# A four-layer graph network in fp32: order of messages and their sums in layers one, three and four

## The chip, the cores and the metric

The kernel runs on one core of one Trainium2 chip. The metric is device time in microseconds (us); the time before is the median of three runs. Inputs and outputs lie in the chip's memory (HBM), and everything is computed in fp32. Engines are named as the profile names them: PE (TensorE), with PEld for its weight loads, DVE (VectorE), ACT (ScalarE), POOL (GpSimd) and SP (SyncE, which issues most DMAs).

## The reference

Sixteen graphs of 1024 nodes with 128 features each go through a graph convolution, a residual and a layer norm, then through a network of four layers, a residual and a layer norm. The four-layer part is what the change is about:

```python
def _layer(nodes, adj, ws, bs, wd, bd, wn, bn, wu, bu):
    src = nodes @ ws + bs
    src_agg = jnp.einsum('bjv,bij->biv', src, _l2norm(adj, 2))
    dst = nodes @ wd + bd
    dst_agg = jnp.einsum('bjv,bji->biv', dst, _l2norm(adj, 1))
    self_rep = nodes @ wn + bn
    upd = jnp.concatenate([src_agg, self_rep, dst_agg], axis=2)
    return jnp.tanh(upd @ wu + bu)
...
for i in range(NUM_LAYERS):
    if i < half:
        stashed.append(fpass)
    elif i == half:
        fpass = jnp.concatenate([fpass, stashed[NUM_LAYERS - i - 1]], axis=2)
    else:
        fpass = jnp.concatenate([fpass, stashed[NUM_LAYERS - i], stashed[NUM_LAYERS - i - 1]], axis=2)
    fpass = _layer(fpass, adj, *params[i])
```

Each node sends a source and a destination message, which are summed over the neighbours with the adjacency matrix (once as it is and once transposed, each normed by rows or columns). The input of layers three and four is two and three blocks of 128 features.

## The kernel before

**Work and order.** The graphs are worked through one after the other, and each engine's order is the order in which the code issues (the scheduling is by hand). While layers one to four of graph b run on TensorE, the other engines prepare graph b+1: they load its adjacency, form its sums of squares, scale and transpose it, and run its first convolution (`first_gnn`) between layers three and four. These pieces hang in `hooks` (issued before a given matmul of `aggregate`) and `between` (issued at numbered places of the messages). The layers are numbered `l` = 0 to 3 in the code, so "layer one" is `l == 0`, "layer three" `l == 2`, "layer four" `l == 3`.

**Messages.** A layer first makes its messages: for each of the eight blocks of 128 nodes the features are the stationary operand and the folded weights stream. They are kept in two SBUF tiles, `t0` (nodes' blocks 0 to 3) and `t1` (blocks 4 to 7). Layers one and two do it in `messages` (L684): a group `g` is two blocks, its product fills one PSUM bank, and DVE evicts it with the bias at L696. The groups come in the order 2, 3, 0, 1, so `t1` is filled first. Layers three and four do it in `paired_messages` (L722), with seven products in place of eight (a Winograd scheme): M4, M1, M2, M3, Z11, Z12 and Z21, where T2, T3 and T4 are differences of halves of the features (L719, L761, L764), and DVE combines the banks at L752, L755 and L758.

**Sums.** The aggregation uses the same seven-product scheme, and for it needs sums of the messages, made by `message_sums` (L702): with X[v, j] the half v of the features in tile `t`j, S3 = X[0,0] - X[1,0], then S1 = X[1,0] + X[1,1], which is written over X[1,0], then S2 = S1 - X[0,0] and S4 = X[0,1] - S2. Every one has a destination part (DST) and a source part (SRC), 256 elements a partition each. S3 is made as two instructions, one for each part (L708), the others as one (L709, L710, L711).

**Aggregation.** `aggregate` (L852) writes its matmuls (L1003) as two lists, `upper` and `lower`, for the upper and the lower 64 columns of the array, and issues them in turn. Each list runs through accumulators in PSUM: in layer one, after products of the node's own features, `upper` begins with M1 (accumulator A, operands X[0,0]) and `lower` with M3 (accumulator Dk, operand S3), then M4 (Ck, S1). In layer four, after the own products, `upper` takes two blocks of M1 and then M2 (Bk, S2), and `lower` two blocks of M4 (S1) and then M3 (S3). In layer three M3 and M4 come after two blocks of Z11. The own products of layers three and four use T2, T3 and T4 once more.

**Buffers.** Four PSUM banks (tag `pt`) serve the messages' products and the accumulators Ck, Dk, A and Bk in rotation. In `messages` all four are filled and evicted in order, and in layer one `aggregate` then takes them in the order Ck, Dk, A, Bk; an accumulator's first matmul waits until the eviction that last read its bank is done. In SBUF, layers three and four keep two scratch tiles, `e0` and `e12` (two halves, `e12[:, 0]` and `e12[:, 1]`). There is one buffer of `e0` for all layers, and the one before layer three is still read by the last tanh of layer two (L1021). T2 lies in `e12[:, 1]`, T4 in `e12[:, 0]`, T3 in `e0`; after the messages and own products, the aggregation uses the tiles for its own results.

**Order of layer three's messages before.** Place 0 (for all graphs but the first and last the three small operations of `inverse_rows`, L395 to L398), M4 and its copy on ACT (L773), M1 and its eviction with bias (L758), then T3 (L761), T4 (L764), then Z12, M2, M3 and the rest.

**Things behind the sums of layer four.** On DVE: `ve` (L452) of the next graph's first norm, which POOL's power (L454) waits for, L459 after that, the next graph's T operations (L680, L676, L678), and the transposes of its rows (L653), the last of which stand right before the evictions of the next graph's layer one.

Of the kernel before, what the change touches and what calls it, by code (L numbers as in the profile page):

```python
# [8 lines left out]
F32 = mybir.dt.float32  # L9
# [5 lines left out]
P = 128  # L15
# [8 lines left out]
def adj_resnorm_kernel(ctx: ExitStack, tc: tile.TileContext, x, adj, w0, b0, layers, out):  # L24
# [33 lines left out]
    nc = tc.nc  # L58
    B, N, D = x.shape
    NB = N // P  # L60
    HW = 512
# [4 lines left out]
    NQ = 4  # L66
# [37 lines left out]
    one = ctx.enter_context(tc.tile_pool(name="one", bufs=1))  # L104
# [38 lines left out]
    def message_seven(wm):  # L143
        return seven(wm, (wm, MSUMS), 2 * P, P)
# [165 lines left out]
    def degree_of(a, state, i, engine=nc.scalar):  # L310
        degree = state["cols"][:, 2 * NB + i:2 * NB + i + 1]
        if engine is nc.vector:
            nc.vector.reduce_sum(degree, a[:, i, :], axis=AX.X)
        else:
# [25 lines left out]
    def column_reduce(b, state, tr):  # L340
        part = two.tile([P, K], F32, tag="part", name=f"part{b}")
        nc.vector.reduce_sum(part, tr.rearrange("p (k r) -> p k r", r=C), axis=AX.X)
        state["part"] = part
# [178 lines left out]
    def first_quarter_3(b, y, T2):  # L522
        T3 = []
        for j in range(2):
# [157 lines left out]
    SRC, DST = 0, 1  # L682

    def messages(b, l, feats, wm, between={}, with_sums=True):  # L684


        nch = CHUNKS[l]
        t = [one.tile([P, NJ, 2, 2, V], F32, tag=f"t{j}", name=f"t{l + 1}_{b}_{j}") for j in range(2)]
        for n, g in enumerate((2, 3, 0, 1)):
            pt = ps_t.tile([P, 2, 2 * P], F32, tag="pt", name=f"pt{l + 1}_{b}_{g}")  # L690
            for q in range(2):
                i = 2 * g + q
                for k, (f, c) in enumerate(feats):
                    by_halves(pt[:, q], f[:, i * P:(i + 1) * P], wm[:, 1 + c], k == 0, k == nch - 1)
            j, o = divmod(2 * g, NJ)
            nc.vector.tensor_add(t[j][:, o:o + 2].rearrange("p k a v c -> p k (a v c)"), pt,  # L696
                                 wm[:, 0][:, None, :].to_broadcast([P, 2, 2 * P]))
            if n in between:
                between[n]()
        return message_sums(b, l, t) if with_sums else t  # L700

    def message_sums(b, l, t):  # L702

        S = {i: one.tile([P, NJ, 2, V], F32, tag=f"S{i}", name=f"S{i}_{l + 1}_{b}") for i in (2, 3, 4)}
        X = {(v, j): t[j][:, :, :, v] for v in range(2) for j in range(2)}
        S[1] = X[1, 0]
        for part in (DST, SRC):
            nc.vector.tensor_sub(S[3][:, :, part], X[0, 0][:, :, part], X[1, 0][:, :, part])  # L708
        nc.vector.tensor_add(S[1], X[1, 0], X[1, 1])  # L709
        nc.vector.tensor_sub(S[2], S[1], X[0, 0])  # L710
        nc.vector.tensor_sub(S[4], X[0, 1], S[2])  # L711
        return X, S

    def begin_paired(b, l, first, second, etag):

        e12 = one.tile([P, 2, HW], F32, tag=etag, name=f"e12_{l}_{b}")
        y = {(j, h): f[:, half(h)] for j, f in enumerate((first, second)) for h in range(NH)}
        w = {"e12": e12, "y": y, "T2": e12[:, 1], "T4": e12[:, 0]}
        nc.vector.tensor_sub(w["T2"], y[1, 1], y[0, 1])  # L719
        return w  # L720

    def paired_messages(b, l, w, wm, rest=None, between={}):  # L722

        t = [one.tile([P, NJ, 2, 2, V], F32, tag=f"t{j}", name=f"t{l + 1}_{b}_{j}") for j in range(2)]
        X = {(v, j): t[j][:, :, :, v] for v in range(2) for j in range(2)}
        y, s, T2, T4 = w["y"], message_seven(wm), w["T2"], w["T4"]
        T3 = w["e0"] = one.tile([P, HW], F32, tag="e0", name=f"e0_{l}_{b}")
        o = own_seven(l, wm)
        w["own"] = {"M1": (o["w00"], y[0, 0]), "M2": (o["S2"], T2), "M3": (o["S3"], T3), "M4": (o["S1"], y[0, 1]),
                    "Z11": (o["w01"], y[1, 0]), "Z12": (o["S4"], y[1, 1]), "Z21": (o["w11"], T4)}  # L730

        def bank(i):
            return product(f"pt{l + 1}_{b}_{i}")

        def parts(pt):
            return pt.rearrange("p (k a c) -> p k a c", k=NJ, a=2)

        def into(pt, *terms):
            for i, (f, x) in enumerate(terms):
                for k in range(NJ):  # L740
                    by_halves(pt[:, k * P:(k + 1) * P], f[:, k * P:(k + 1) * P], x, i == k == 0,
                              i == len(terms) - 1 and k == NJ - 1)
            return pt

        def plain(v, h):
            return [(rest[:, half(h)], wm[:, MREST + v * P:MREST + (v + 1) * P])] if rest is not None else []

        def bias(v):
            return wm[:, v * P:(v + 1) * P].rearrange("p (a c) -> p a c", a=2)[:, None].to_broadcast([P, NJ, 2, V])

        def add(to, x, pt):
            nc.vector.tensor_add(X[to], X[x], parts(pt))  # L752

        def add_sbuf(to, x):
            nc.vector.tensor_add(X[to], X[to], X[x])  # L755

        def add_bias(to, x, v):
            nc.vector.tensor_add(X[to], x, bias(v))  # L758

        def t3():  # L760
            nc.vector.tensor_sub(T3, T2, y[0, 0])  # L761

        def t4():
            nc.vector.tensor_sub(T4, y[1, 0], T2)  # L764

        def at(i):
            if i in between:
                between[i]()

        if l == 2:  # L770
            at(0)
            m4 = into(bank(4), (y[0, 1], s["S1"]))
            nc.scalar.copy(X[1, 1], parts(m4))  # L773
            m1 = into(bank(1), (y[0, 0], s["w00"]))
            add_bias((0, 0), parts(m1), 0)
            t3()
            t4()
            z12 = into(bank("z12"), (y[1, 1], s["S4"]))
            m2 = into(bank(2), (T2, s["S2"]))
            at(1)  # L780
            add((0, 1), (0, 0), m2)
            m3 = into(bank(3), (T3, s["S3"]))
            add((1, 0), (0, 1), m3)
            add_sbuf((0, 1), (1, 1))
            at(2)
            add((0, 1), (0, 1), z12)
            z11 = into(bank("z11"), (y[1, 0], s["w01"]))
            add((0, 0), (0, 0), z11)
            z21 = into(small(f"pt{l + 1}_{b}_z21", [HW]), (T4, s["w11"]))
            add_bias((1, 0), X[1, 0], 1)  # L790
            add_sbuf((1, 1), (1, 0))
            add((1, 0), (1, 0), z21)
        else:
            t4()
            t3()
            m4 = into(bank(4), (y[0, 1], s["S1"]))
            nc.scalar.copy(X[1, 1], parts(m4))
            at(0)
            m1 = into(bank(1), (y[0, 0], s["w00"]))
            add_bias((0, 0), parts(m1), 0)  # L800
            at(1)
            m2 = into(bank(2), (T2, s["S2"]))
            add((0, 1), (0, 0), m2)
            at(2)
            z11 = into(bank("z11"), (y[1, 0], s["w01"]), *plain(0, 0))
            m3 = into(bank(3), (T3, s["S3"]))
            add((1, 0), (0, 1), m3)
            add_bias((1, 0), X[1, 0], 1)
            z12 = into(bank("z12"), (y[1, 1], s["S4"]), *plain(0, 1))
            add_sbuf((0, 1), (1, 1))  # L810
            at(3)
            add((0, 0), (0, 0), z11)
            add_sbuf((1, 1), (1, 0))
            add((0, 1), (0, 1), z12)
            z21 = into(small(f"pt{l + 1}_{b}_z21", [HW]), (T4, s["w11"]), *plain(1, 0))
            add((1, 0), (1, 0), z21)
            p11 = into(bank("p11"), *plain(1, 1))
            add((1, 1), (1, 1), p11)
            at(4)
        XS = message_sums(b, l, t)  # L820
        if l == 2:
            at(3)
        return XS

    def plain_layer(b, l, feats, t, wm, a, at, fT, etag, hooks):
# [279 lines left out]
    wm = message_tile("wm1_0")  # L1105
# [10 lines left out]
    wm = as_chunks(wm, 0)  # L1116
# [11 lines left out]
    for p in (3, 4):  # L1128
        v = one.tile([P, NJ, HW], F32, tag=f"T{p}", name=f"sq0_{p}").rearrange("p k i -> p (k i)")
# [131 lines left out]
    for b in range(B):  # L1261
        nxt = b + 1 < B
        n = b + 1
        y, yt = quarters(a), quarters_t(at)
# [5 lines left out]
        if b == 0:  # L1270
# [17 lines left out]
            t = messages(b, 0, feats, wm, {0: second_x1, 1: factors_and_fold, 2: row_factors0}, with_sums=False)  # L1288
# [47 lines left out]
            wm = message_weights(b, 1)  # L1336
            a2 = load(n)
            xs2 = load_spread(n)
        else:
            w = {}  # L1340
            if nxt:
                st = begin_sums(n)
            t = messages(b, 0, feats, wm)
# [30 lines left out]
            wm = ahead["wm"]  # L1374
# [5 lines left out]
        t = messages(b, 1, feats, wm)  # L1380
# [23 lines left out]
        else:  # L1404
            nm = f"1_{b - 1}"
            w = {"ys": summed(f"y{nm}", "xa")}
# [34 lines left out]
        wm = ahead["wm"]  # L1441
# [5 lines left out]
        w = {}  # L1447
# [54 lines left out]
        t = paired_messages(b, 2, p, wm, None, between)  # L1502
# [9 lines left out]
        wm = ahead["wm"]  # L1512
# [8 lines left out]
        if nxt:  # L1521
            nm = f"0_{n}"
            xT2 = w["xT"]
            w = {}
# [102 lines left out]
        t = paired_messages(b, 3, p, wm, f23, between)  # L1627
        if nxt:
            wm = message_weights(n, 0)
# [10 lines left out]
    b = B - 1  # L1640
# [48 lines left out]
```

## Time and profile before

| what | value |
|---|---|
| median of three runs | 2396.12 us (2395.91 to 2396.41) |
| the profiled execution's own time | 2395.86 us |
| its span, first to last instruction | 2394.1 us |
| granted TensorE clock | 0.999 |
| matmuls of the aggregation, L1003, in the chain that ended last | m 40%, z 28%, m3s 1% of the span |
| matmuls of the messages, L245, in that chain | pt 9%, pt_z 5%, pt_p 1% |
| DVE in that chain | 1% |
| mean of one L709, L710 or L711 (128x512) | 692 ns |
| mean of one L708 (128x256) | 420 ns |
| mean of one L696 eviction (128x512 out of PSUM) | 684 ns |
| mean of one power on POOL, L454 | 6396 ns |

The span is the profiler's; the time is the run's own, 1.8 us longer. Busy time of PE is a union of matmuls whose ends are modelled, so it is read together with the start times. In the timeline a line merges consecutive instructions of one kind: start of the first, time to the end of the last, their number, and in brackets the engine's idle time before it with what ended it. A line of the stretches gives the length, then for each engine its busy time and number of instructions.

### The profile page before, as it was taken

How to read it: one execution, taken by the hardware profiler on the slowest of the kernel's cores; microseconds unless marked ns; L12 is line 12 of the kernel's file. 1: busy time of each engine (PE TensorE's matmuls, PEld its weight loads, DVE VectorE, ACT ScalarE, POOL GpSimd, SP SyncE). 2: the span in 40 equal slices, each digit the busy share in tenths (PEclk: the TensorE clock that was granted, in tenths of full speed). 3: DMA queues.
4: the chain of work that ended last, by engine and by line, in shares of the span. 5: the costliest groups of instructions: out<-in, count | busy, mean ns of one | idle time of the engine just before them, and what ended most of it. 6: DMA issues, size and time to landing. Idle time of an engine off the chain costs nothing.

```text
span 2394.1 us, 39329 instructions
## 1 busy us (share of the span) xinstructions
PE 2377.4 (99%) x15289; PEld 1279.6 (53%) x15289; DVE 2092.6 (87%) x2817; ACT 980.8 (41%) x1845; POOL 275.8 (12%) x103
## 2 busy tenths in 40 slices
PE   8999999999999999999999999999999999999998
PEld 4444564645556455554655546456464554645555
DVE  6998888999889989889988889888898988998954
ACT  5425345253343524435244452434525344352322
POOL 4101111001111011110111110111100111101110
PEclk9999999999999999999999999999999999999999
DMA  9527244262533627335272442634427253362400
GB/s 205 124 75 147 69 115 90 70 148 57 135 78 81 138 48 157 61 97 115 55 163 55 108 97 71 147 69 110 91 70 151 57 133 76 80 141 48 100 22 22
DMA packets 363387, 232.03 MB, mean 97 GB/s; under 512 B 150353, under 2 KB 334306, under 8 KB 363202
## 3 DMA queue, kind: packets, MB, share of 16 engines
q1 hardware_dynamic: 362386, 227.03, 42.5%
q0 software_dynamic: 816, 2.49, 0.4%
q8 instruction: 121, 1.98, 0.4%
q14 instruction: 64, 0.52, 0.1%
HBM read 209.59 MB, written 19.84 MB: 96 GB/s over the span
## 4 chain that ended last, share of the span: by engine, by line
PE 92%; DVE 1%; issue 0%; POOLq 0%; ACT 0%; DVEq 0%
PE m L1003 40%; PE z L1003 28%; PE pt L245 9%; PE pt_z L245 5%; PE m_f L581 5%; PE z_f L581 2%; PE pw L245 2%; PE m3s L1003 1%; PE pt_p L245 1%; DVE t L752 0%; PE pv L250 0%; PE pm L250 0%; DVE f L534 0%; PE rp L250 0%; DVE t L758 0%
## 5 line engine op out<-in xcount | busy, mean ns | idle before, releaser
L1003 PE MATMUL m<-a,t 128*64 128x512 f32 x1008 | 434.7, 593 | 0.2 <-DVE t L709 0.2
L1003 PE MATMUL m<-at,t 128*64 128x512 f32 x1008 | 418.6, 592 | 0.0
L1003 PE MATMUL m<-Q,S 128*64 128x512 f32 x880 | 394.0, 593 | 0.0
L1003 PE MATMUL m<-T,S 128*64 128x512 f32 (+1 forms) x1040 | 393.6, 573 | 0.0
L454 POOL TENSOR_TENSOR rs<-ve,mhalf 128x32 f32<-128x32 f32 x30 | 191.9, 6396 | 988.4 <-DVE ve L452 988.4
L1003 PE MATMUL z<-at,t 128*64 128x512 f32 x504 | 229.2, 592 | 0.0
L1003 PE MATMUL z<-at,S 128*64 128x512 f32 x504 | 228.3, 593 | 0.0
L1003 PE MATMUL z<-a,S 128*64 128x512 f32 x504 | 228.2, 593 | 0.0
L1003 PE MATMUL z<-a,t 128*64 128x512 f32 x504 | 227.2, 593 | 0.0
L1003 PE MATMUL z<-Q,t 128*64 128x512 f32 x504 | 227.0, 593 | 0.0
L1003 PEld LDWEIGHTS m<-T,S 128*64 128x64 f32 x1040 | 131.3, 137 | 129.5 <-issue 127.6
L1003 PEld LDWEIGHTS m<-Q,S 128*64 128x64 f32 x880 | 118.2, 137 | 150.4 <-issue 143.0
L1003 PEld LDWEIGHTS m<-at,t 128*64 128x64 f32 x1008 | 131.6, 137 | 110.7 <-issue 109.4
L1003 PEld LDWEIGHTS m<-a,t 128*64 128x64 f32 x1008 | 132.0, 137 | 109.8 <-issue 101.0
L1003 PE MATMUL z<-T,t 128*64 128x512 f32 x384 | 172.8, 592 | 0.0
L882 ACT COPY e<-m 64x512 f32<-64x512 f32 x63 | 36.7, 582 | 327.4 <-PE m L1003 327.0
L374 POOL TENSOR_TENSOR inv<-cols,mhalf 128x16 f32<-128x16 f32 (+1 forms) x17 | 46.8, 2751 | 1033.3 <-DVE cols L373 1033.3
L412 DVE TENSOR_TENSOR a<-a,cinv 128x512 f32<-128x512 f32 x250 | 155.6, 696 | 0.8 <-DMA xn<-in_x_dram 0.8
L320 ACT ACTIVATE sq<-a 128x1024 f32<-128x1024 f32 x120 | 125.9, 1050 | 37.0 <-DVE acc L327 23.1
L245 PE MATMUL pt<-wm,f1T 128*64 128x128 f32 (+1 forms) x1536 | 134.3, 309 | 1.2 <-ACT f1T L1021 1.2
L245 PEld LDWEIGHTS pt<-wm,f1T 128*64 128x64 f32 x1536 | 109.1, 137 | 34.6 <-issue 12.3
L315 ACT ACTIVATE a<-a 128x1024 f32<-128x1024 f32 x120 | 125.3, 1045 | 0.4
(309 smaller groups left out, 5023.3 us busy)
## 6 DMA issues: line engine op xcount, KB each, us to landing
a<-in_adj_dram SPq DMA_DIRECT2D x120, 512.0 KB
rows<-in_adj_dram SPq DMA_DIRECT2D x480, 64.0 KB
a<-in_adj_dram SPq DMA_DIRECT2D x240, 128.0 KB
wm<-wsave SPq DMA_DIRECT2D x32, 704.0 KB
wm<-wsave SPq DMA_DIRECT2D x31, 320.0 KB
xn<-in_x_dram SPq DMA_DIRECT2D x124, 64.0 KB
xs<-in_x_dram SPq DMA_DIRECT2D x60, 128.0 KB
cinv<-dr SPq DMA_DIRECT2D x30, 256.0 KB
```

The source lines that it names most:

```text
L245: nc.tensor.matmul(out[s], x[:, s], y, start=start, stop=stop)
L315: nc.scalar.activation(a[:, i, :], a[:, i, :], AF.Copy, accum_out=degree)
L320: nc.scalar.activation(sq, a[:, i, :], AF.Square, accum_out=state["cols"][:, i:i + 1])
L374: nc.gpsimd.tensor_tensor(inv[:, s], cols[:, s], mhalf[:, s], ALU.pow)
L412: engine.tensor_mul(a[:, i, s], a[:, i, s], cinv[:, s])
L454: nc.gpsimd.tensor_tensor(rstd, ve, mhalf[:, :n], ALU.pow)
L581: nc.tensor.matmul(o, x_, y_, start=start, stop=stop)
L882: nc.scalar.copy(e0[high], A[high])
L1003: nc.tensor.matmul(o, x, y_, start=start, stop=stop)
```

## The change

Three edits, all in the helpers of the messages.

1. In layer one of all graphs but the first, the groups are made in the order 0, 1, 2, 3, and the two instructions of S3 are issued after the second group's eviction, since both of S3's operands lie in `t0`. S1, S2 and S4 stay after the fourth. (The first graph's layer one takes another path and keeps its order; layer two keeps order and sums.)
2. In layer three, T3 is put in `e12[:, 0]` and T4 in `e0`, and T3 is issued right after place 0, before M4's copy and M1's eviction.
3. In layer four, S3 and S1 are made by parts in turn: S3's DST, S1's DST, S3's SRC, S1's SRC, then S2 and S4. S1 is thus two instructions in place of one. Layer three's sums stay as they were.

The tiles of S2, S3 and S4 are now made by `sums_tiles`, in `messages` ahead of the loop.

```diff
-        for n, g in enumerate((2, 3, 0, 1)):
+        S, X = sums_tiles(b, l, t) if with_sums else (None, None)
+        for n, g in enumerate((2, 3, 0, 1) if l or b == 0 else range(NQ)):
...
+            if l == 0 and with_sums and n == 1:
+                sums_3(X, S)
+        if not with_sums:
+            return t
+        if l:
+            sums_3(X, S)
+        return message_sums(X, S)
+
+    def sums_tiles(b, l, t):
 
         S = {i: one.tile([P, NJ, 2, V], F32, tag=f"S{i}", name=f"S{i}_{l + 1}_{b}") for i in (2, 3, 4)}
-        X = {(v, j): t[j][:, :, :, v] for v in range(2) for j in range(2)}
+        return S, {(v, j): t[j][:, :, :, v] for v in range(2) for j in range(2)}
+
+    def sums_3(X, S, parts=(DST, SRC)):
+        for part in parts:
+            nc.vector.tensor_sub(S[3][:, :, part], X[0, 0][:, :, part], X[1, 0][:, :, part])
+
+    def message_sums(X, S, parts=()):
+
         S[1] = X[1, 0]
-        for part in (DST, SRC):
-            nc.vector.tensor_sub(S[3][:, :, part], X[0, 0][:, :, part], X[1, 0][:, :, part])
-        nc.vector.tensor_add(S[1], X[1, 0], X[1, 1])
+        for part in parts:
+            sums_3(X, S, (part,))
+            nc.vector.tensor_add(S[1][:, :, part], X[1, 0][:, :, part], X[1, 1][:, :, part])
+        if not parts:
+            nc.vector.tensor_add(S[1], X[1, 0], X[1, 1])
         nc.vector.tensor_sub(S[2], S[1], X[0, 0])
         nc.vector.tensor_sub(S[4], X[0, 1], S[2])
...
-        T3 = w["e0"] = one.tile([P, HW], F32, tag="e0", name=f"e0_{l}_{b}")
+        e0 = w["e0"] = one.tile([P, HW], F32, tag="e0", name=f"e0_{l}_{b}")
+        T3, T4 = (w["e12"][:, 0], e0) if l == 2 else (e0, w["e12"][:, 0])
...
         if l == 2:
             at(0)
+            t3()
             m4 = into(bank(4), (y[0, 1], s["S1"]))
             nc.scalar.copy(X[1, 1], parts(m4))
             m1 = into(bank(1), (y[0, 0], s["w00"]))
             add_bias((0, 0), parts(m1), 0)
-            t3()
             t4()
...
-        XS = message_sums(b, l, t)
+        S, _ = sums_tiles(b, l, t)
         if l == 2:
+            sums_3(X, S)
+            XS = message_sums(X, S)
             at(3)
+        else:
+            XS = message_sums(X, S, (DST, SRC))
```

More of the change, by code (lines that the diff above doesn't have):

```diff
@@ L699, in messages @@
                 between[n]()
-        return message_sums(b, l, t) if with_sums else t
-    def message_sums(b, l, t):
-        S = {i: one.tile([P, NJ, 2, V], F32, tag=f"S{i}", name=f"S{i}_{l + 1}_{b}") for i in (2, 3, 4)}
-        X = {(v, j): t[j][:, :, :, v] for v in range(2) for j in range(2)}
-        S[1] = X[1, 0]
-        for part in (DST, SRC):
-            nc.vector.tensor_sub(S[3][:, :, part], X[0, 0][:, :, part], X[1, 0][:, :, part])
-        nc.vector.tensor_add(S[1], X[1, 0], X[1, 1])
+            if l == 0 and with_sums and n == 1:
[6 more added lines that the diff above has]
+    def sums_tiles(b, l, t):
+        S = {i: one.tile([P, NJ, 2, V], F32, tag=f"S{i}", name=f"S{i}_{l + 1}_{b}") for i in (2, 3, 4)}
+        return S, {(v, j): t[j][:, :, :, v] for v in range(2) for j in range(2)}
[3 more added lines that the diff above has]
+    def message_sums(X, S, parts=()):
+        S[1] = X[1, 0]
+        for part in parts:
[3 more added lines that the diff above has]
+            nc.vector.tensor_add(S[1], X[1, 0], X[1, 1])
         nc.vector.tensor_sub(S[2], S[1], X[0, 0])
@@ L717, in begin_paired @@
         y = {(j, h): f[:, half(h)] for j, f in enumerate((first, second)) for h in range(NH)}
-        w = {"e12": e12, "y": y, "T2": e12[:, 1], "T4": e12[:, 0]}
+        w = {"e12": e12, "y": y, "T2": e12[:, 1]}
         nc.vector.tensor_sub(w["T2"], y[1, 1], y[0, 1])
@@ L725, in paired_messages @@
         X = {(v, j): t[j][:, :, :, v] for v in range(2) for j in range(2)}
-        y, s, T2, T4 = w["y"], message_seven(wm), w["T2"], w["T4"]
-        T3 = w["e0"] = one.tile([P, HW], F32, tag="e0", name=f"e0_{l}_{b}")
+        y, s, T2 = w["y"], message_seven(wm), w["T2"]
+        e0 = w["e0"] = one.tile([P, HW], F32, tag="e0", name=f"e0_{l}_{b}")
+        T3, T4 = (w["e12"][:, 0], e0) if l == 2 else (e0, w["e12"][:, 0])
         o = own_seven(l, wm)
```

## The prediction

> **What bounds the kernel now.** I read the page first, then one steady graph alone, then the three places that the diff touches in the timeline. The page's engine rows, and a stretch as long as one graph:
>
> ```profile
> PE 2377.4 (99%) x15289; PEld 1279.6 (53%) x15289; DVE 2092.6 (87%) x2817; ACT 980.8 (41%) x1845; POOL 275.8 (12%) x103
> ...
> 326.20:472.65 146.45, 146.45 (x953) 79.42 (x952) 131.85 (x176) 60.01 (x112) 15.68 (x4) 1.00 0.44 97
> ```
>
> TensorE is the bound, 146.45 us for each graph. But 99% says only that some matmul is always under way. Every product is issued twice, for the upper and the lower 64 columns of the array, and each half (I call it a lane) keeps its own pace:
>
> ```profile
> 486.06 0.59 PE L1003 MATMUL z<-at,S 128*64 128x512 f32 x1
> 486.13 0.59 PE L1003 MATMUL m<-Q,S 128*64 128x512 f32 x1
> 486.49 0.59 PE L1003 MATMUL z<-at,S 128*64 128x512 f32 x1
> 486.56 0.59 PE L1003 MATMUL m<-Q,S 128*64 128x512 f32 x1
> ```
>
> A pass of 512 columns comes every 0.43 us in each lane, of 128 columns every 0.11. A lane can stand for 0.3 us while the other hides it from the busy share. So I compared start times in each lane with these paces. In a steady graph three stalls stand out, and the diff touches all three.
>
> Layer four (DVE, then PE):
>
> ```profile
> 471.11 0.75 DVE L708 TENSOR_TENSOR S<-t 128x256 f32<-128x256 f32 x2
> 471.89 0.69 DVE L709 TENSOR_TENSOR t<-t,t 128x512 f32<-128x512 f32 x1
> ...
> 471.85 0.68 PE L1003 MATMUL m<-e,wx 128*64 128x512 f32 x2
> ...
> 472.73 1.04 PE L1003 MATMUL m<-a,t 128*64 128x512 f32 x3
> ```
>
> S1 (L709) ends at 472.58; the first matmul of M4 starts at 472.73, which prices the way from a DVE end to a matmul at 0.15. The lower lane's last own pass began at 471.94 (the second of the two; they end 0.68 after 471.85), plus 0.43, plus two short passes of pv of 0.03: it was free at 472.42. **Lower lane, 0.31 us.**
>
> Layer one:
>
> ```profile
> 355.45 0.76 DVE L708 TENSOR_TENSOR S<-t 128x256 f32<-128x256 f32 x2
> ...
> 355.60 1.02 PE L1003 MATMUL m<-a,t 128*64 128x512 f32 x2
> 356.02 0.61 PE L1003 MATMUL m<-T,S 128*64 128x512 f32 x1
> ```
>
> The first half of S3 takes 0.42, ends at 355.88, plus 0.15: exactly M3's start at 356.02. The lane was free at 355.95. **Lower lane, 0.07.**
>
> Layer three:
>
> ```profile
> 410.87 0.21 DVE L398 STREAM_TRANSPOSE invt<-inv 128x32 f32<-128x32 f32 x1
> 411.58 0.69 DVE L758 TENSOR_TENSOR t<-pt,wm 128x512 f32<-128x512 f32 x1 [0.50 <-PE pt L245]
> 412.19 0.68 DVE L761 TENSOR_TENSOR e<-e,f1T 128x512 f32<-128x512 f32 x1
> ...
> 411.87 0.27 PE L245 MATMUL pt<-wm,e 128*64 128x128 f32 x1
> ...
> 412.20 0.33 PE L245 MATMUL pt<-wm,e 128*64 128x128 f32 x2
> ```
>
> M2's product starts at 411.87 in the upper lane and 0.33 later, at 412.20, in the lower one: the lag that the two stalls above made (0.38) is still there. Eight passes on (8 x 0.109), at 412.74, the upper lane wants M3, but T3 (L761) ends at 412.87 and with 0.15 M3 starts at 413.02. **Upper lane, 0.27-0.28**, just while the lower one catches up. So the three are two sides of one loss: per graph the lower lane stands 0.38 and the upper 0.27, and neither side pays alone.
>
> **What the Trainium skill says.** "TensorEngine Tiling (Array Packing)", Key Properties: column tiles operate independently, loads and matmuls in parallel. The trace agrees: the stalls above are in one lane only. "TensorE: Matmul & The Clock Gate", Part 3 (what overlaps): matmuls start in program order. I take both: the lanes run on, but a lane can lead only by what is queued, so a lead is paid back. "VectorE: DVE Perf Modes", The TRN2 errata: an fp32 tensor_tensor of N elements takes (N+151)/0.96 ns, so halving an operation costs a fixed part twice; the trace has 0.69 for 512 and 0.42 for 256. No page prices the lag between lanes.
>
> **Layer four, S3 and S1 by parts.** Now: S3 first half 471.11-471.53, S1 first half after it (it overwrites what S3 reads, so it starts 0.03 after the end, as S1 does now) 471.56-471.98, S3 second half 471.90-472.32 (independent, 0.34 after), S1 second half 472.35-472.77, S2 472.80-473.49, S4 473.53-474.22. M4's first half is ready at 471.98 + 0.15 = 472.13, before 472.42: the 0.31 goes, with 0.29 to spare. Cost: four halves instead of two and a whole, so S2, S4 and ve behind them come 0.18 later. S2's first use is 474.08 (upper lane, four passes after 472.37); 473.49 + 0.15 is in time. ve starts the POOL power (7.34 us) whose end releases L459 at 481.66, so this and T's 2.25 us operation come 0.18 later, to 486.57; the transposes behind wait until 487.18 anyway.
>
> **Layer three, T3 and T4.** The same two subtractions swap buffers; none is added. T3 no longer waits for the tanh that reads e0, and stands ahead of L758. DVE idles 0.50 there: T3 runs 411.0-411.7, L758 slips from 411.58 to about 411.6, T4 (e0 is free once the tanh ends, 411.28, which T4 needs anyway) ends near 412.9. T3 is ready at 411.85 against 412.74: the 0.27 goes. Next late is M3's eviction chain (L752 on), PE-fed, and S3 of this layer: now 419.57 + 0.15 against a use at 420.04; if TensorE comes 0.27 earlier and this chain nearly not, 0.05 is left. Tight, no stall. ACT and the DMA queues issue nothing new.
>
> **Layer one, block order.** S3 needs only t0, now evicted first and second; then the two halves of S3, then evictions three and four. From 352.95 at 0.60 apiece: evictions to 353.55 and 354.22, S3 354.26-355.02, third 354.94-355.62, fourth to 356.22, S1 at 356.25 as now. S3's 0.07 goes. The added wait: product M1 takes the third of the four PSUM banks, so its first matmul now waits for the third eviction, 355.62 + 0.15 = 355.77 instead of 355.60, and all TensorE behind it. That would be 0.17. But the DVE stream that ends in these evictions starts with the transposes held until 487.18 (one graph earlier for this one, 340.74), and what holds them is the lower lane: its last product from the transposed adjacency starts at 486.49, ends 0.59 later. Without the 0.31 that is at 486.9, still after 486.57. So evictions come about 0.28 earlier against the upper lane, the bank is free at 355.49, and 0.1 is to spare. I take 0 for it and keep 0.17.
>
> **The sum.** Graphs two to sixteen: between 0.27 (upper lane) and 0.38 (lower); some small gaps of the upper lane beside the lag (0.06 at the start of layer three) should close too, so I take 0.33. Fourteen graphs give 4.6. The first graph differs: its first half of S1 comes 0.61 before where S1 ends now (L709 at 179.71, to 179.10), of which, with the second graph's stalls, I count 0.7; its T3 stall of 0.99 mostly moves to the adds behind the wait for POOL's inv (0.90), but T4 ahead of L366 moves that chain up by 117.01 - 116.73 = 0.28. In all 5.6 us. Against the profiled execution: span 2394.1 to 2388.5, with the 1.8 around it 2390.3; that run stands 0.3 below the median, so 2390.5 in the timed runs.
>
> **Rivals.**
> 1. Main course, 2390.5: 0.60.
> 2. Layer one's bank keeps its wait, since the transposes don't come earlier: 0.17 and maybe the 0.18 of ve on top, say 0.2 per graph, leaves 0.13 x 14 + 1 = 2.8: 2393.3. For it: third eviction and S3 share one in-order queue; against: the lower lane's times above. 0.18.
> 3. The lag is free: the queue lets one lane lead, and a small gap elsewhere pays it, so only the first graph gains: 2395. For it: no view shows both lanes idle. Against: T3's stall in the other lane, equal to the lag. Also here: a part that doesn't act, as T3 still held by something else. 0.14.
> 4. Slower: one mechanism, the third bank of layer one. If S3 waits long behind the second eviction and the whole DVE stream of layer four comes 0.18 and more late, M1 starts at 356.2, 0.6 late, in both lanes. It decides once the third eviction ends more than 0.33 after 355.45, at 355.78 on before's clock. 15 x (0.6 - 0.33) - 1 = +3.1: 2399, and up to 2402. For it: DVE shows no idle from 348 to 360. 0.08.
>
> **How the numbers follow.** About 0.2% (4.8 us) is what a measurement of this kernel can tell: faster means below 2391.3. The main case's own range is 2388.8 to 2392.0 (0.22 to 0.42 a graph and the first graph's 0 to 1.5); about 0.85 of it lies below. Faster 0.60 x 0.9 + 0.18 x 0.15, with a little off for tight margins = 0.56; slower by 0.2% half of rival 4 and a little for what I don't see = 0.06; the rest, 0.38, is within. The range of 8 in 10 takes rival 2 and part of 3: 2388.8 to 2395.0.
>
> **What would show it.** In the changed trace: M4's first matmul in layer four follows pv without a hole; the M3 product of layer three follows M2 at 0.11; L708 stands between two pairs of L696; a steady graph takes about 146.1 instead of 146.45. Wrong if M1's first matmul in layer one starts 0.15 after the third eviction (rival 2 or 4), or if the holes are gone and the period is the same (rival 3): then another wait holds one lane.

## The result, and the profile after

The changed kernel takes 2390.93 us (median of 22 runs, 2389.48 to 2396.16) against 2396.36 us before, measured beside it. The ratio is 0.9979, with a 95% interval of 0.9972 to 0.9985: faster by 0.21%. The prediction was 2390.5. The span of the profiled execution is 2388.4 us (2388.5 predicted), at the same granted clock, 0.999.

The page's engine rows of the changed kernel:

```profile
PE 2373.0 (99%) x15289; PEld 1606.8 (67%) x15289; DVE 2095.0 (88%) x2833; ACT 980.3 (41%) x1845; POOL 275.7 (12%) x103
```

And one steady graph of it, as a stretch (length, then busy time and instructions of PE, PEld, DVE, ACT, POOL, then clock, DMA share, GB/s):

```profile
471.60:617.67 146.07, 146.07 (x957) 101.16 (x954) 132.01 (x177) 62.76 (x118) 15.68 (x4) 1.00 0.44 99
```

PE is busy for the whole of its 146.07 us, as it was for the whole of 146.45. The busy share can't show what was won; the length of the graph can. I measure that length from the first matmul of the readout product `pw` on `e_f` in one graph to the same matmul in the next. It repeats within 0.02 us: 146.44 before, 146.07 now. So a graph won 0.37 us.

From these start times the whole difference of the spans adds up. Thirteen such periods give 13 x 0.37 = 4.8. The first period, which has the first graph's layer four and the second graph's layers one to three in it, went from 148.23 to 147.36: 0.87. The first readout came 0.2 later, and what follows the last one is 0.2 shorter. 4.8 + 0.87 - 0.2 + 0.2 = 5.7, against 2394.1 - 2388.4 = 5.7.

The 0.2 hides two larger numbers. The first graph's layer three (its first message product that reads T2) began at 115.49 where it began at 114.47, 1.0 later, and from there to the first readout it takes 46.60 us where it took 47.42. That start lies anywhere from 114.38 to 115.95 in the ten executions of these two kernels and of the variants below that leave out some of the edits, so the 1.0 is scatter.

The three places of before, in the changed kernel. Layer four, DVE in the timeline (S3 is now L716, S1 by parts L723, S2 L726, S4 L727):

```profile
470.69 0.42 DVE L723 TENSOR_TENSOR t<-t,t 128x256 f32<-128x256 f32 x1
471.04 0.41 DVE L716 TENSOR_TENSOR S<-t 128x256 f32<-128x256 f32 x1
471.49 0.43 DVE L723 TENSOR_TENSOR t<-t,t 128x256 f32<-128x256 f32 x1
471.95 0.69 DVE L726 TENSOR_TENSOR S<-t 128x512 f32<-128x512 f32 x1
```

and PE there (the aggregation's matmul is now L1024):

```profile
470.65 1.02 PE L1024 MATMUL m<-e,wx 128*64 128x512 f32 x3
471.25 0.25 PE L250 MATMUL pv<-v,fold 128*64 128x32 f32 x2
471.33 0.62 PE L1024 MATMUL m<-a,t 128*64 128x512 f32 x1
471.50 0.25 PE L250 MATMUL pv<-v,fold 128*64 128x32 f32 x2
471.59 1.91 PE L1024 MATMUL m<-a,t 128*64 128x512 f32 x7
```

S1's first half ends at 471.11, and with the prediction's 0.15 from there to a matmul it is ready at 471.26. The lower lane's M4 starts at 471.59, 0.06 behind the second of its two `pv` (471.53): it waits for nothing, with 0.33 to spare.

Layer one, DVE and then PE (the eviction is now L697, S1 in one piece L725):

```profile
498.25 1.27 DVE L697 TENSOR_TENSOR t<-pt,wm 128x512 f32<-128x512 f32 x2
499.56 0.76 DVE L716 TENSOR_TENSOR S<-t 128x256 f32<-128x256 f32 x2
500.24 1.28 DVE L697 TENSOR_TENSOR t<-pt,wm 128x512 f32<-128x512 f32 x2
501.55 0.69 DVE L725 TENSOR_TENSOR t<-t,t 128x512 f32<-128x512 f32 x1
```

```profile
501.00 0.59 PE L1024 MATMUL m<-a,t 128*64 128x512 f32 x1
501.26 0.59 PE L1024 MATMUL m<-T,S 128*64 128x512 f32 x1
```

S3 stands between two pairs of evictions, and its second half ends at 500.32, almost a microsecond before M3 (`m<-T,S`) starts.

Layer three, DVE and then PE (M1's eviction is now L775, T3 L778, T4 L781):

```profile
556.08 0.21 DVE L398 STREAM_TRANSPOSE invt<-inv 128x32 f32<-128x32 f32 x1
556.22 0.65 DVE L778 TENSOR_TENSOR e<-e,f1T 128x512 f32<-128x512 f32 x1
556.79 0.69 DVE L775 TENSOR_TENSOR t<-pt,wm 128x512 f32<-128x512 f32 x1
557.40 0.68 DVE L781 TENSOR_TENSOR e<-f23T,e 128x512 f32<-128x512 f32 x1
```

```profile
557.20 0.27 PE L245 MATMUL pt<-wm,e 128*64 128x128 f32 x1
...
557.42 1.73 PE L245 MATMUL pt<-wm,e 128*64 128x128 f32 x28
```

T3 is done at 556.87; M2 starts at 557.20 and runs on into M3. The idle 0.50 ahead of M1's eviction is filled.

All three stalls are gone. What is left in each lane are the small steps at the short norm sums (about 0.06 each, in two parts) and a few nanoseconds per matmul: from 466 to 614 no matmul of either lane starts more than 0.05 us behind its lane's pace. The lower lane still starts M2 0.26 behind the upper one (557.46), and that costs nothing: a lag is no loss as long as neither lane stands.

### The profile page after: what moved, and what is told of

Same layout as the page of the kernel before. It is cut to its first block, busy times and chain, and to the rows that moved or that the text cites. A ratio compares the mean times of both kernels' runs of the same rounds, so it can differ in the third digit from the quotient of the medians.

```text
span 2388.4 us, 39344 instructions
## 1 busy us (share of the span) xinstructions
PE 2373.0 (99%) x15289; PEld 1606.8 (67%) x15289; DVE 2095.0 (88%) x2833; ACT 980.3 (41%) x1845; POOL 275.7 (12%) x103
## 4 chain that ended last, share of the span: by engine, by line
PE 95%; DVE 2%; DMA 2%; SPq 0%; issue 0%; ACT 0%; POOLq 0%; DVEq 0%
PE m L1024 35%; PE z L1024 34%; PE pt L245 9%; PE pt_z L245 5%; PE m_f L581 4%; PE z_f L581 4%; PE pw L245 2%; PE m3s L1024 1%; DMA wm<-in_L_gnn_ws_dram 1%; PE pt_p L245 1%; DMA Q<-in_adj_dram 1%; DMA raw<-in_L_gnn_wu_dram 0%; DVE acc L329 0%; DVE at L653 0%; DMA a<-in_adj_dram 0%
## 5 line engine op out<-in xcount | busy, mean ns | idle before, releaser
L1024 PE MATMUL m<-a,t 128*64 128x512 f32 x1008 | 434.7, 593 | 0.0
L1024 PE MATMUL m<-at,t 128*64 128x512 f32 x1008 | 420.5, 593 | 0.0
L1024 PE MATMUL m<-T,S 128*64 128x512 f32 (+1 forms) x1040 | 399.1, 573 | 0.0
L1024 PE MATMUL m<-Q,S 128*64 128x512 f32 x880 | 394.0, 593 | 0.0
L1024 PE MATMUL z<-at,t 128*64 128x512 f32 x504 | 229.2, 592 | 0.0
L1024 PE MATMUL z<-at,S 128*64 128x512 f32 x504 | 228.3, 593 | 0.0
L1024 PE MATMUL z<-a,S 128*64 128x512 f32 x504 | 228.2, 593 | 0.0
L1024 PE MATMUL z<-a,t 128*64 128x512 f32 x504 | 227.2, 593 | 0.0
L1024 PE MATMUL z<-Q,t 128*64 128x512 f32 x504 | 227.0, 593 | 0.0
L1024 PEld LDWEIGHTS m<-T,S 128*64 128x64 f32 x1040 | 142.0, 137 | 76.4 <-issue 3.7
L1024 PEld LDWEIGHTS m<-at,t 128*64 128x64 f32 x1008 | 137.0, 137 | 76.9 <-issue 4.6
L1024 PEld LDWEIGHTS m<-a,t 128*64 128x64 f32 x1008 | 134.4, 137 | 77.5 <-issue 9.2
L1024 PE MATMUL z<-T,t 128*64 128x512 f32 x384 | 172.8, 592 | 0.0
L1024 PEld LDWEIGHTS m<-Q,S 128*64 128x64 f32 x880 | 118.2, 137 | 33.0 <-issue 4.6
L245 PEld LDWEIGHTS pt<-wm,f1T 128*64 128x64 f32 x1536 | 115.6, 137 | 23.2 <-ACT f1T L1042 6.0
```

The lines of the kernel that those rows point to most:

```text
L245: nc.tensor.matmul(out[s], x[:, s], y, start=start, stop=stop)
L1024: nc.tensor.matmul(o, x, y_, start=start, stop=stop)
```

## The experiments

Three theories stood against each other. **A**: the lower lane's stalls (at S1 in layer four and at S3 in layer one) set the pace, and T3's stall in the upper lane only echoes the lag that they leave. **B**, as predicted: the three are two sides of one loss, and neither side pays alone. **C**: each stall counts by itself.

**Each edit alone.** Three kernels have one edit and leave out the other two. The T3 edit alone:

```diff
-        T3 = w["e0"] = one.tile([P, HW], F32, tag="e0", name=f"e0_{l}_{b}")
+        e0 = w["e0"] = one.tile([P, HW], F32, tag="e0", name=f"e0_{l}_{b}")
+        T3, T4 = (w["e12"][:, 0], e0) if l == 2 else (e0, w["e12"][:, 0])
...
             at(0)
+            t3()
...
-            t3()
             t4()
```

> Only layer three's edit (T3 in the free half of e12 and issued sooner). Steady graph before 146.43 us, changed kernel 146.07. Theory A (the lower lane's stalls set the pace, T3's stall in the upper lane only echoes its lag): T3's stall goes, the upper lane waits elsewhere, 146.38 to 146.45, time within 1 us of before. Theory B (as predicted: two sides, neither pays alone): the same, 146.38 to 146.45. Theory C (each stall counts for itself): 0.27 less, 146.16, time 4 us less.

The graph stayed at 146.44, and the time at 2396.09. T3's stall is gone, and the upper lane waits elsewhere. PE at the start of layer two's messages:

```profile
525.49 0.59 PE L1022 MATMUL z<-at,t 128*64 128x512 f32 x1
525.82 0.43 PE L245 MATMUL pt<-wm,f1T 128*64 128x256 f32 x1
525.91 0.59 PE L1022 MATMUL z<-at,t 128*64 128x512 f32 x1
526.09 1.28 PE L245 MATMUL pt<-wm,f1T 128*64 128x256 f32 x9
```

The lower lane is still in the last `z` product (525.91) while the upper one begins the messages at 525.82, 0.12 late, and goes on at 526.09, another 0.05 late. Three more such gaps stand at 556.06 (0.06) and in layer four's messages near 611.4 (0.12 and 0.06). The lower lane still stands 0.31 at S1 and 0.08 at S3.

Layer four's parts alone:

```diff
-        XS = message_sums(b, l, t)
+        S, _ = sums_tiles(b, l, t)
         if l == 2:
+            sums_3(X, S)
+            XS = message_sums(X, S)
             at(3)
+        else:
+            XS = message_sums(X, S, (DST, SRC))
```

> Only layer four's sums by parts. Theory A: without the 0.31 of S1 the lower lane lags less, Z0's last product and so L1010, the tanh and T3 come about 0.28 earlier against the upper lane, and T3's stall shrinks to nothing by itself: steady graph 146.10 to 146.20, time 4 to 5 us under before. Theory B: the upper lane's 0.27 at T3 stays and sets the pace: 146.38 to 146.45. Theory C: 0.31 less, 146.12, with T3's stall of 0.27 still in the trace.

The graph fell to 146.17 and the time to 2392.07. T3 was not touched, and yet its stall shrank from 0.27 to 0.08.

Layer one's order alone:

```diff
-        for n, g in enumerate((2, 3, 0, 1)):
+        for n, g in enumerate((2, 3, 0, 1) if l or b == 0 else range(NQ)):
...
+            if l == 0 and with_sums and n == 1:
+                sums_3(X, S)
```

> Only layer one's order. The third bank is evicted behind S3, and with layer four as before the transposes don't come earlier, so M1 should start about 0.17 late in layer one (rival 2's wait, seen alone). Theory A: the upper lane has room for it (it led by the lag), T3's stall shrinks by as much, and S3's 0.07 goes: 146.35 to 146.45. Theory B: the same to a few hundredths. Theory C: 146.43 + 0.17 - 0.07 = 146.53 or more.

The graph fell to 146.35, the time to 2394.95. S3's stall is gone, and T3's fell only to 0.25, as the lower lane still stands 0.31 at S1. The wait that I had expected at M1 isn't there. DVE, then PE, of this kernel:

```profile
501.24 1.28 DVE L697 TENSOR_TENSOR t<-pt,wm 128x512 f32<-128x512 f32 x2
```

```profile
501.90 0.59 PE L1025 MATMUL m<-a,t 128*64 128x512 f32 x1
```

The third eviction starts at 501.24 and takes 0.68, to 501.92. M1 starts at 501.90, before it is over. So M1 doesn't take that eviction's bank.

**Each edit taken out of the changed kernel.** Without T3's:

```diff
-        T3, T4 = (w["e12"][:, 0], e0) if l == 2 else (e0, w["e12"][:, 0])
+        T3, T4 = e0, w["e12"][:, 0]
...
             at(0)
-            t3()
...
+            t3()
             t4()
```

> The changed kernel with layer three's edit undone (layers one and four changed). Theory A: T3's stall is gone though T3 stands where it stood: 146.07 to 146.12, time as the changed kernel's within 1 us apart from the first graph's T3. Theory B: T3's stall of 0.27 stays: 146.3 to 146.4. Theory C: 146.07 + 0.27 = 146.34.

2390.76, the graph at 146.07: nothing is lost. DVE in layer three of this kernel, and PE beside it:

```profile
556.43 0.21 DVE L398 STREAM_TRANSPOSE invt<-inv 128x32 f32<-128x32 f32 x1
557.14 0.69 DVE L775 TENSOR_TENSOR t<-pt,wm 128x512 f32<-128x512 f32 x1 [0.50 <-PE pt L245]
557.75 0.68 DVE L778 TENSOR_TENSOR e<-e,f1T 128x512 f32<-128x512 f32 x1
```

```profile
557.73 2.00 PE L245 MATMUL pt<-wm,e 128*64 128x128 f32 x32
```

T3 stands where it stood, behind M1's eviction, and M2 and M3 run through in one line of 32 matmuls without a hole. The lanes start M2 0.09 apart (before: 0.38). M1's eviction reads both halves of the bank, so it waits for the lane that is behind. With less lag it starts 0.59 before M2 does in the upper lane (557.14 against 557.73), where it started 0.29 before (411.58 against 411.87). T3 comes right behind it and is ready at 558.58; M3 is wanted at 557.73 + 0.87 = 558.60. T3 was late because the lower lane was. The four kernels that leave T3 in its old place show it by size: the lag at M2 is 0.38 (before), 0.36 (layer one's edit alone), 0.19 (layer four's alone) and 0.09 (both), and the upper lane stands 0.27, 0.25, 0.08 and 0 at M3. As long as it stands at all, that is the lag less 0.11.

The pair was run a second time, the changed kernel and the one without T3's edit.

> The changed kernel once more, beside the next two on one chip: 2390 to 2391.5, steady graph 146.07.

> Layer three's edit undone. If T3's stall only echoed the lower lane's lag, the edit is worth the first graph alone, 0 to 0.5 us: 2390.0 to 2392.0, steady graph 146.07. If it is worth its 0.27 a graph, 2394 to 2395.

2390.62 and 2390.87, both graphs at 146.07 again. The one repeated difference is in the first period: 147.36 and 147.37 with T3's edit, 147.54 and 147.55 without. Most of it is a stall of 0.15 at T3 in the second graph's layer three. In the first graph's layer three the edit does what the prediction's sum said: from the operation that makes T2 to L366 DVE takes 3.00 us in each of five executions with it and 3.28 in each of five without. So it is worth 0.18 and 0.28 us, each once in the whole run, and the medians of the two pairs (2390.93 and 2390.62 with it, 2390.76 and 2390.87 without) are too close to show it.

Without layer one's order:

```diff
-        for n, g in enumerate((2, 3, 0, 1) if l or b == 0 else range(NQ)):
+        for n, g in enumerate((2, 3, 0, 1)):
...
-            if l == 0 and with_sums and n == 1:
-                sums_3(X, S)
...
-        if l:
-            sums_3(X, S)
+        sums_3(X, S)
```

> Layer one's edit undone, layers three and four changed. Lower lane's stalls alone set the pace: S3's 0.07 to 0.09 stays, 146.15 to 146.17 as with layer four's edit alone, 1.2 to 1.4 us over the changed kernel. If layer one's edit were worth nothing: 146.07.

The graph is at 146.17, the time 2391.74. S3's 0.07 is back in the lower lane, and the upper one waits 0.10 in layer four's messages.

Without layer four's parts:

```diff
-            XS = message_sums(X, S, (DST, SRC))
+            sums_3(X, S)
+            XS = message_sums(X, S)
```

> The changed kernel without the layer-four edit (S3's two halves, then S1 whole, as before); layer one's order and the T3 edit stay. A (the lower lane's stalls set the pace, T3's is an echo): the lower lane still stands 0.31 a graph at M4, so the graph stays where layer one's edit alone had it, 146.34, and the time near 2394.7; the upper lane pays about 0.27 in other places, since T3 is no longer what it waits for. B (no side pays alone, all three are needed): no gain at all in the steady graphs, 146.44. C (each stall counts by itself, T3's 0.27 among them): 146.07 + 0.31 minus nothing for T3 and S3, so near 146.1 to 146.15.

The graph is at 146.35, the time 2394.83. The lower lane stands 0.31 at M4. The upper one waits 0.13 and 0.05 at the start of layer two's messages and 0.10 in layer four's.

So all eight combinations are measured:

| edits in the kernel | graph, us | time, us | ratio to before, 95% interval |
|---|---|---|---|
| none | 146.439 | 2396.36 | |
| T3 | 146.440 | 2396.09 | 0.9999 (0.9990 to 1.0007) |
| layer one | 146.346 | 2394.95 | 0.9991 (0.9982 to 0.9999) |
| layer one, T3 | 146.348 | 2394.83 | 0.9994 (0.9985 to 1.0002) |
| layer four | 146.167 | 2392.07 | 0.9981 (0.9973 to 0.9988) |
| layer four, T3 | 146.167 | 2391.74 | 0.9979 (0.9970 to 0.9988) |
| layer four, layer one | 146.073 | 2390.76 | 0.9976 (0.9968 to 0.9985) |
| all three | 146.073 | 2390.93 | 0.9979 (0.9972 to 0.9985) |

The graph is the mean of the thirteen periods, which lie within 0.03 of one another in each of these kernels. The times alone don't tell neighbouring rows apart; the graphs do. Layer four's edit is worth 0.27 a graph, layer one's 0.09, T3's nothing, whatever else is there. The two sum to the 0.37 (0.273 + 0.093). That is theory A on every row. B needs the single edits to win nothing, and C needs T3's edit to win 0.27.

**How much a stall of the lower lane costs.** The changed kernel, with half an S3 (the same subtraction once more, into the same place) put ahead of layer four's sums, once and three times:

```diff
         else:
+            sums_3(X, S, (DST,))
             XS = message_sums(X, S, (DST, SRC))
```

> The changed kernel with one half-width DVE operation (S3's destination part once more) ahead of layer four's sums, 0.34 to 0.45 us. Theory A with the working's slack of 0.29: S1's first half comes 0.05 to 0.16 too late, the lower lane stands so long, the steady graph grows by that, 146.12 to 146.23. If the lag were free (rival 3): 146.07. If there were no slack: 146.45.

> The same with three such operations, 1.0 to 1.35 us. Theory A: the lower lane stands 0.75 to 1.05, more than a lane can lead, so the upper one waits as well, and the graph grows by about the lower lane's stall, 146.8 to 147.1; T3's stall in layer three comes back in the upper lane. Rival 3: 146.07 to 146.4.

One more half: the lower lane stands 0.17 at M4 and most graphs take 146.205, which is 0.13 more. Three more (`(DST,) * 3`): it stands 1.11, and a graph takes 147.125. From the one to the other the stall grew by 0.94 and the graph by 0.92, nearly its whole length. The single runs took 2393.11 and 2406.02. I had expected T3's stall to come back with three, and it didn't: in this kernel T3 is made early. What did come is a stall in the upper lane too. PE there:

```profile
473.45 0.62 PE L1025 MATMUL m<-a,t 128*64 128x512 f32 x1
473.62 0.25 PE L250 MATMUL pv<-v,fold 128*64 128x32 f32 x2
473.91 0.59 PE L1025 MATMUL m<-a,t 128*64 128x512 f32 x1
474.78 1.90 PE L1025 MATMUL m<-a,t 128*64 128x512 f32 x6 [0.28 <-DVE t L723]
```

The upper lane runs two passes of M1 (473.45, 473.91). Its third would be due at 474.34, and comes at 474.78, in the moment in which the lower lane's M4 starts. M1 doesn't read S1. Its two blocks are four passes here, so the first two passes are one matmul of the code, and the next is issued behind M4's first. The delay also reaches S2, which the upper lane's M2 reads: with three it stands 0.51 more there, and 0.08 with one. So these two runs delay both lanes. Their sizes agree with theory A, but they don't prove it; the single edits do, where the upper lane's M2 waits for nothing.

**Is the third bank of layer one a danger?** The changed kernel with S3 made twice in layer one, so that the third and fourth evictions come later:

```diff
             if l == 0 and with_sums and n == 1:
                 sums_3(X, S)
+                sums_3(X, S)
```

> The changed kernel with S3 made twice in layer one, so the third and fourth evictions come 0.7 to 0.8 us later. If M1 takes the third group's bank, as the working had it: M1 starts 0.6 late in layer one in every graph but the first, 146.4 to 146.7. If M1 takes a bank that was evicted before S3, as layer one's order alone suggests (M1 started while the third eviction still ran): no stall at M1, 146.07 to 146.12.

The graph went to 146.39 and the time to 2394.88, but not by a wait at M1. DVE and PE:

```profile
500.49 1.43 DVE L717 TENSOR_TENSOR S<-t 128x256 f32<-128x256 f32 x4
501.84 1.28 DVE L697 TENSOR_TENSOR t<-pt,wm 128x512 f32<-128x512 f32 x2
```

```profile
502.17 0.59 PE L1025 MATMUL m<-a,t 128*64 128x512 f32 x1
502.17 0.59 PE L1025 MATMUL m<-T,S 128*64 128x512 f32 x1
```

The third eviction runs from 501.84 to about 502.5, and M1 starts at 502.17 in the middle of it. In the program as built, M1's accumulator lies in the bank that the first group left, M3's in the second's, M2's in the third's and M4's in the fourth's: the banks don't go round in the order in which they are asked for. The 0.31 is lost at the end of layer one. DVE, ACT and PE there, in the changed kernel:

```profile
523.36 0.69 DVE L921 TENSOR_TENSOR e<-e 128x512 f32<-128x512 f32 x1
...
524.09 0.72 ACT L1042 ACTIVATE f1T<-e,bout 128x512 f32<-128x512 f32 x1 [0.90 <-DVE e L921]
...
525.03 2.80 PE L245 MATMUL pt<-wm,f1T 128*64 128x256 f32 x23
```

and with S3 made twice:

```profile
524.96 0.69 DVE L922 TENSOR_TENSOR e<-e 128x512 f32<-128x512 f32 x1
...
525.69 0.72 ACT L1043 ACTIVATE f1T<-e,bout 128x512 f32<-128x512 f32 x1 [0.90 <-DVE e L922]
...
526.46 1.73 PE L245 MATMUL pt<-wm,f1T 128*64 128x256 f32 x14
```

The first messages of layer two read the first tanh of layer one (on ACT), which waits for an add on DVE. From the third eviction to this add DVE takes 23.12 us in both kernels, and the third eviction stands 0.67 further behind S3's start (1.35 against 0.68). In the changed kernel the tanh ends at 524.81 and its first message starts at 525.03. With S3 made twice it ends at 526.41, the message starts 0.05 later, and both lanes have stood 0.26 to 0.27 for it (the rest goes at the next pass). The order of the evictions cost nothing; the DVE chain to this tanh is what is next late, with 0.22 - 0.05 = 0.17 us to spare. This is one run of the kernel, and the graph's length, the same within 0.01 in all thirteen periods, carries the reading.

**The first graph.** The changed kernel has its largest stalls in the first graph, one of them (1.64 us) at M1 in layer three's aggregation, on a DVE chain that stands 0.91 for POOL's inverse. One kernel moves the factors' step by one group:

```diff
-                between = {1: inverses3, 2: factors}
+                between = {1: inverses3, 3: factors}
```

> The changed kernel with one line moved in the first graph: the inverse rows of layer three (which wait for POOL's power) are issued after the layer's sums instead of amid its adds. DVE's wait of 0.9 us and three small operations leave the way to M1 in layer three: its stall of 1.64 us shrinks to 0.2 to 0.4, 1.2 to 1.4 us less once, 2389.6, unless the row of factors then comes too late for the scaling that follows (then about 0, or 1 to 3 us more). Steady graphs unchanged, 146.07.

2395.28, ratio 0.9994 (0.9986 to 1.0002): the gain of the change is given back. The stall at M1 is gone, and of the 0.55 at M3 behind it 0.23 is left, but the factors are then late for the next stage. PE:

```profile
147.24 1.02 PE L581 MATMUL m_f<-a,xn 128*64 128x512 f32 x2
152.08 4.88 PE L581 MATMUL m_f<-a,xn 128*64 128x512 f32 x13 [3.82 <-DVE xn L510]
```

Both lanes stand from 148.26 to 152.08. The steady graph is 146.07 as before. No version tried here beats the changed kernel; the one without T3's edit is as fast.

## Why the prediction held, and where it didn't

**The total.** 5.6 us was predicted; the medians differ by 5.4 and the spans by 5.7. The terms are not quite those of the sum. The steady graphs gave more than the 4.6 written down: 4.8 for the thirteen full periods and 0.2 after the last readout, since a graph gained 0.37 and not 0.33. I had taken a value between the two lanes' stalls, 0.27 and 0.38. The lower lane's was the right one. The first graph and the first period gave what was written or a little more: 0.28 in layer three, and 0.87 where 0.7 was put. That the spans come so near to the forecast is partly luck: the changed kernel's execution began its first layer three 1.0 later and then won 0.8 up to the first readout, of which only the 0.28 is explained.

**Layer four** went by its steps: 0.29 to spare was worked out and 0.33 is there; S2, S4 and what follows are 0.2 later and nobody waits for them.

**Layer three.** T3 is early, as said, but that isn't where the time was. The sentence that failed is that the three are two sides of one loss and "neither side pays alone". The upper lane's 0.27 was the echo of the lower lane's 0.38: M1's eviction, on which T3 followed, waits for the lane that is behind. (The working read that lag as 0.33. The matmul at 412.20 is the upper lane's fourth of M2; the lower lane's first is at 412.25, 0.38 behind.) With the lag gone T3 is in time in its old place; with T3 early and the lag still there, the upper lane loses the same time elsewhere. I saw the lag and its size, and took the second stall for a second cause.

**Layer one.** The step "product M1 takes the third of the four PSUM banks" is wrong; it takes the first. The 0.17 that I feared, and the rivals 2 and 4 built on it, had no mechanism. The forecast took 0 for it, for another reason than the real one. The small slack that does exist, 0.17, lies at the end of layer one.

**Rival 3**, that the lag is free, is half right. A steady lag is free: the changed kernel keeps 0.26 at M2 and the one without T3's edit 0.09, with the same graph. The stalls that make it are not: layer four's edit alone takes away one stall of the lower lane and wins 0.27, and in the lateness runs a growth of that stall by 0.94 goes with 0.92.

**The size of a stall.** The 0.31 of layer four was taken too large. M4 follows the second `pv` at 0.06 where nothing holds it (471.53 to 471.59), and not at the 0.03 of the working, so 0.28 could be won, and 0.27 was. In the same way the 0.17 of the run with one more half is 0.14, and cost 0.13. Layer one's 0.07 was taken too small: behind a late M3 the lane's next pass comes at 0.45 and not at 0.43, so it is worth 0.09.

**The odds.** The sum for "faster" uses 0.9 for the main case where the line before it has 0.85; with 0.85 it is 0.54 and not 0.57.

**Left open.** That the first period's gains don't add up over the single edits (0.60 for layer four's, 0.44 for layer one's and 0.27 for T3's alone, against 0.87 for all) wasn't pursued.

## What to carry to other kernels

Where two independent streams share an engine, compare each stream's start times with its own pace, and ask of every stall whether the stream that waits is behind or ahead: a stall of the one ahead may only be the other's lag coming back, and removing it moves the wait. Try each edit alone and each one taken out; it took both to show that one of three is worth nothing in the steady graphs. Size a stall against the same steps where nothing waits. Read which buffer an instruction really takes from start times before a wait on it goes into a forecast.

## What was not expected of the hardware

- A lag between the two column halves is kept for long: the 0.31 from S1 in layer four and the 0.07 from S3 in layer one are still there as 0.38 at M2 in layer three of the next graph, while both halves run at full pace. "TensorEngine Tiling (Array Packing)", Key Properties, of the Trainium skill says that the tiles operate independently. The runs agree up to a bound: with a stall of 1.11 us in one half, the other ran on for two passes and then stood 0.44 us too, though its own operand was there. Its next matmul comes behind the waiting one in the code's order, and the prediction had taken that matmuls start in that order. For single passes the order doesn't hold: in layer four before, M4's first pass starts at 472.73, ahead of the second pass of M1's first matmul at 472.83, whose weights were loaded 0.31 before M4's (472.40, 472.70).
- The way from the end of a DVE operation to the matmul that waits for it isn't one figure: 0.15 at M4 behind S1 (472.58 to 472.73, before), 0.05 at M2 behind S2 with three more halves (476.15 to 476.20).
- The busy time of weight loads rose from 1279.6 to 1606.8 us with the same 15289 loads and a shorter run. Over the kernels here it lies between 1043.0 (S3 made twice in layer one, where the starts shown above fall together) and 1613.9 (the factors' step moved), and two kernels with the same graph of 146.07 have 1415.8 and 1606.8. It goes with how the loads of the two halves overlap, I take it, and is no measure of load work here.
